# Moving the Toeplitz loads into the last pass, the raw tap loads forward, and the inverse transforms onto one PSUM tile

## The chip, the cores and the metric

One program runs on one core of a Trainium2 chip. The metric is the device time of one execution in microseconds (us). Three runs of the kernel before took 2757.65, 2760.22 and 2761.01 us; the median is 2760.22. A separate execution was recorded by the hardware profiler: it took 2763.0 us, and the span from its first to its last instruction was 2761.2 us.

Engines are named as in the profile: PE is the matrix engine (PEld its weight loads), DVE the vector engine, ACT the scalar engine, POOL the GpSimd engine, SP the engine that only issues DMAs. A row with a q (SPq, ACTq) is the engine's sequencer, which waits and issues.

## The reference, cut to what matters

Four residual layers act on `x` of shape (4, 32, 32, 16): `x = x + conv(_gn(x))` with a group norm `_gn` over 8 groups of 2 channels. The first three layers have the same form:

```
first   = einsum('ijpq,bpqc->bijc', M, inputs)
K       = G as a 3x3 kernel with 16 input and 32*32*16 output channels
shifted = conv3x3(inputs, K).reshape(b, h, w, h, w, f)
diff    = relu(inputs[:, :, :, None, None, :] - shifted)
second  = einsum('ijpq,bpqijc->bijc', Wp, diff)
return first - second
```

So each of the 1024 places (i, j) has nine taps of 16x16 and one 32x32 map of weights. `G` is 9.4 MB and `Wp` 4.2 MB per layer; `Wp` is repeated over 16 channels on its way in. The fourth layer is a convolution with an impulse response:

```
H = rfft2(numerators) / rfft2(denumerator)    # 32 x 32 points here
h = irfft2(H)                                 # the impulse response, 16 x 16 channels
y = irfft2(rfft2(x, 64x64) * (h0 + rfft2(h, 64x64)))[:32, :32]
```

which is a zero-padded linear convolution of the normed input with `h`, plus `h0` at the origin.

## The kernel before, in words

**Conv layers.** The 1024 places of a layer are 128 blocks of 8 places by 16 channels. An iteration is one block for one batch; there are 1536 of them, listed in `order` (L110) in five passes per layer: the first 12 or 16 blocks for batches 0 and 1, the same blocks backwards for batches 2 and 3, the middle blocks for all four batches, then the last 12 or 16 blocks for batches 0 and 1 and, backwards, for 2 and 3. Layer 2 ends with 12 blocks, so its last pass has 24 iterations. An iteration (L740) makes six products that two kinds of pixel share (L704, one iteration ahead), lets ACT copy them beside themselves (L713) and clear the other half of a later tile (L662), adds twelve products of its own (L731), and DVE takes the minimum with zero, multiplies with the block's W and sums, in one instruction (L753). PSUM is four tiles of two banks, used in turn (`pair_psum`, L57). A tile that never served anything else keeps its PE accumulate flags (`full`); one that did has to be written over by two matmuls (L658) before ACT may clear it. The first 24 iterations take another way (`direct`, L671).

**What an iteration needs.** Four blocks make a use (`uses`, `begin`). A use needs an F tile of four taps (L518, three slots f0 to f2), and a taps tile `g` of the others (L574, 1.5 MB, three slots g0 to g2). The latter is made by `other_taps` (L536): SP loads a raw tile (L544; two buffers), POOL subtracts, adds (L510, L549), splits it in a rounded part and the rest (L553, L555; one buffer for the rounded part) and stores both four times over in DRAM (`gd`, L559); `piece_loads` (L568) loads the result into the slot. W tiles are 1 MB for two blocks, in a ring of six (L601 to L629).

**Order of the work.** Every engine runs its instructions in the order in which the program wrote them (`manual_schedule`). The side work is a set of generators. After every iteration `step` (L633) advances each by one `yield`: `todo` has what follows a norm, `tasks` the loads in order of their due times (L586 to L599), which are iteration numbers compared with `now["at"]`. A generator `beside` goes on once a block in a layer's middle pass, and `also` once a block in its last one. SP's DMAs stand in one queue: an issue that waits for a buffer or for another DMA holds up all that is written behind it. The same is true of POOL, which computes as well.

**Layer 3 beside the others.** In the middle pass of layer 0 `impulse_response` (L819) divides the coefficients' transforms and inverts the result in two steps: 64 matmuls into two PSUM tiles (L872) with two ACT copies (L883) and eight stores (L887), then 32 matmuls into two PSUM tiles (L913), two copies (L922), sixteen POOL copies (L928) and a store of `hd`. From `hd` a convolution is a product with Toeplitz tiles k = 0 to 7: one tile is 128 x 4 x 16 x 40 values, 1.31 MB, in which eight groups of 16 partitions hold the same rows shifted; `load_toeplitz` (L942) writes one DMA for each group, odd and even ones on two queues. Tiles 1, 7 and 6 are loaded into a pool of three (`tp`) and tile 0 into one more (`tp2`) in layer 2's middle pass, tile 5 in its last pass, in halves of two W tiles (`late_toeplitz`, L1143). When layer 2 is done, the last norm runs (`norm3`, L1065) and the tail begins (L1158): groups of 16 matmuls (`run`, L1050) over the tiles in the order 1, 0, 7, 6, 5, 4, 3, 2, 0. Tiles 4, 3 and 2 are loaded there, on SP and ACT (L1164 to L1166), each into the `tp` buffer that the matmuls have just left. Beside this, `side` holds the products of pairs of row blocks: ACT copies it out of PSUM (L1169), POOL stores it (L1175) and loads it in another order (L1177, `both`), as it does with the input itself (`xq`, `xd`, `xo`: L1119, L1124, L1159). DVE adds all of it to `xo` (L1181, L1188, L1194), and the two halves of the output are stored (L1200).

Of the kernel before, what the change touches and what calls it, by code (L numbers as in the profile page):

```python
# [7 lines left out]
F32 = mybir.dt.float32  # L8
# [17 lines left out]
GC = 4  # L26
# [11 lines left out]
def conv_stack_kernel(ctx, tc, x, M, W, raw_f, first_g, F, E, h0, coef, cst, dft, idp, idq, out):  # L38
# [497 lines left out]
    def other_taps(q, at):  # L536

        layer, ch = divmod(q, NBLK // GC)
        yield from until(at[0])
        while len(raws) > 1 and stored.get(raws[-2], now["at"]) + 8 > now["at"]:  # L540
            yield
        raws.append(q)
        raw = er.tile([96, 3, 2 * P], F32, tag="raw", name="raw")
        nc.sync.dma_start(out=raw.rearrange("r k n -> r (k n)"), in_=E[layer][ch])  # L544
# [23 lines left out]
    def piece_loads(u, q, slot, free):  # L568

        yield from until(max(free, begin[u] - 12))  # L570
        while q not in stored:
            yield
        gt[q] = t = taps_tile(slot)
        nc.sync.dma_start(  # L574
            out=t.rearrange("p d u s n -> p (d u s n)").bitcast(F32),
            in_=gd[q % len(gd)].rearrange("a k (c d) x -> (a k c) (d x)", d=6),
        )
# [12 lines left out]
    for q in reversed(qs):  # L590
        ready[q] = last = max(min(need[q] - 32, last - 14), 0)
    for q in qs:
        load = max(0, done[-2] + 8, ready[q] - 20)
        at = load, max(ready[q], done[-1] + 1, load + (8 if q else 3))
        done.append(at[1] + 6)
        tasks.append((load, other_taps(q, at)))
    tasks += [(begin[load[0]] - 30, four_taps(n)) for n, load in enumerate(f_plan) if n]
# [10 lines left out]
    def w_free():  # L608
        return any(last is not None and last <= now["at"] for last in ring)
# [209 lines left out]
    def impulse_response():  # L819


        with tc.tile_pool(name="fs", bufs=1) as fs, tc.tile_pool(name="ft", bufs=1) as ft:
            table = fs.tile([P, 2, NF - SOON * P], F32, name="table")
            inv = fs.tile([P, 2, 2, 2 * S], F32, name="inv")
            for h in range(2):
                nc.gpsimd.dma_start(out=table[64 * h : 64 * h + 64], in_=dft)
            nc.gpsimd.dma_start(out=inv, in_=idp)
            H = fs.tile([P, NCH, 2, 2 * P], F32, name="H")
            for ch in range(NCH):
                if ch < SOON:  # L830
                    s = soon[ch]
                else:
                    pab = next_psum()
                    for ri in range(2):
                        coefficient_dft(pab, ab, table[:, :, bass.ts(ch - SOON, P)], ri)
                    s = ft.tile([P, 2, 2, 2 * P], F32, name="s")
# [12 lines left out]
                mul(hr, br, ar)  # L849
                mul(t, bi, ai)  # L850
                nc.gpsimd.tensor_tensor(hr, hr, t, ALU.add)
                mul(hr, hr, d)
                mul(hi, bi, ar)
                mul(t, br, ai)
                nc.gpsimd.tensor_tensor(hi, hi, t, ALU.subtract)
                mul(hi, hi, d)
                yield
                if ch == 0:

                    for ri, one_over in enumerate((d[:2], t[:2])):  # L860
                        nc.vector.reciprocal(one_over, s[:2, 0, ri])
                        mul(H[:2, ch, ri], s[:2, 1, ri], one_over)
                    yield


            pks = [pair_psum() for _ in range(2)]
            for pair in range(2):
                for ri in range(2):
                    for ch in (2 * pair, 2 * pair + 1):
                        for r in range(4):  # L870
                            rows = slice(S * r, S * r + S)
                            nc.tensor.matmul(  # L872
                                pks[r // 2][bass.ts(ch % 2, 64), r % 2, bass.ts(pair, 2 * P)],
                                lhsT=inv[rows, int(ch == 0), ri],
                                rhs=H[rows, ch, ri],
                                start=ri == 0,
                                stop=ri == 1,
                            )

            parts = []  # L880
            for n, pk in enumerate(pks):
                parts.append(H[:, bass.ts(n, 2)].rearrange("p c r n -> p c (r n)"))
                nc.scalar.copy(parts[n], pk)  # L883
            for n, part in enumerate(parts):
                for ch in range(NCH):
                    kx, half = 4 * ch + 2 * n, 64 * (ch % 2)
                    nc.gpsimd.dma_start(  # L887
                        out=td[kx : kx + 2].rearrange("k r p n -> (r p) k n"),
                        in_=part[half : half + 64, :, bass.ts(ch // 2, 2 * P)],
                    )  # L890
                yield


        with tc.tile_pool(name="fs2", bufs=1) as fs:
# [11 lines left out]
                nc.gpsimd.dma_start(out=v[g : g + 32], in_=rows[u])  # L906
            for _ in range(6):
                yield
            pq = [pair_psum() for _ in range(2)]
            quarter = [slice(32 * u, 32 * u + 32) for u in range(4)]  # L910
            for u in range(4):
                for c in range(4):
                    nc.tensor.matmul(  # L913
                        pq[u // 2][quarter[c], u % 2, :],
                        lhsT=inv[quarter[u]],
                        rhs=v[quarter[u], bass.ts(c, 8)].rearrange("g p m -> g (p m)"),
                        start=True,
                        stop=True,
                    )

            for n in range(2):
                nc.scalar.copy(  # L922
                    v[:, bass.ts(n, 16)].rearrange("q (u p) m -> q u (p m)", u=2), pq[n]
                )
            yield
            for u in range(4):
                for c in range(4):
                    nc.gpsimd.tensor_copy(  # L928
                        hs[quarter[u], :, bass.ts(c, 8)],
                        v[quarter[c], bass.ts(u, 8)].rearrange("q p m -> q m p"),  # L930
                    )
                yield
            nc.gpsimd.tensor_tensor(hs[:, :, 0], hs[:, :, 0], h0s, ALU.add)
# [5 lines left out]
                )  # L939
            yield  # L940

    def load_toeplitz(k, *parts, other=nc.gpsimd):  # L942


        n = C * PITCH
        for p in range(8):
            start = 8 + k * TQ * n - p
            for t in parts:
                src = hd[start:]
                size = t.shape[1] * n  # L950
                (nc.sync, other)[p % 2].dma_start(  # L951
                    out=t[p * C : (p + 1) * C].rearrange("i q j r -> i (q j r)"),
                    in_=bass.AP(src.tensor, src.offset, [[HLEN, C], [1, size]]),
                )
# [187 lines left out]

    def late_toeplitz():  # L1143

        half = TQ // 2 * C * PITCH
        parts = []
        for _ in range(2):
            while not w_free():
                yield
            wt = w_tile(len(order)).rearrange("p k m -> p (k m)")  # L1150
            parts.append(wt[:, :half].rearrange("p (q j r) -> p q j r", j=C, r=PITCH))
        ts[held[-1]] = [part[:, q] for part in parts for q in range(TQ // 2)]
        yield from load_toeplitz(held[-1], *parts)

    xs = conv_layer(2, xs, norm3, toeplitz(), late_toeplitz())
    drain()
# [4 lines left out]
    pt = pair_psum()  # L1161
    bank_of.update({1: pt[:, 0], 2: pt[:, 1]})
    for n, slot in enumerate(then):
        if n in (2, 4, 5):  # L1164
            k = {2: 4, 4: 3, 5: last}[n]
            list(load_toeplitz(k, toeplitz_tile(k, late["tp"]), other=nc.scalar))  # L1166
        if n == 3:
            side = junkp.tile([P, 2, S * C], F32, tag="junk", name="side")
            nc.scalar.copy(  # L1169
# [169 lines left out]
```

## Time and profile before

| what | value |
|---|---|
| median of three runs | 2760.22 us |
| profiled execution, and its span | 2763.0 us, 2761.2 us |
| PE, DVE, ACT, POOL busy | 98%, 70%, 64%, 30% of the span |
| one iteration in the steady state, by DVE's starts | 1.69 us |
| Toeplitz tiles 4, 3 and 2 in the tail: first issue, and last landing of each | 2710.09; 2722.94, 2735.60, 2746.08 us |
| DMA, all queues | 652 MB, mean 236 GB/s |

A PE that is 98% busy can still be late: a matmul that runs at half the clock is twice as long, and a tail of 60 us weighs 2% of the whole. So the stages have to be looked at one by one. A row of the timeline gives start, duration, engine, line, operation, tiles as out<-in, and shape; what stands in brackets is the engine's idle time before it and what ended it. A row of the chain of waits gives start, duration and what the end of the program was waiting for just then. Windows give the busy time of each engine in a stretch, the clock that PE was granted (1.00 is all of it), the share of time in which the 16 DMA engines were busy, and the rate.

### The profile page before, as it was taken

Reading aid. Unit: us, or ns where it says so; the run is one execution under the profiler, and the core shown is the slowest. Engines: PE = TensorE matmul, PEld = TensorE weight load, DVE = VectorE, ACT = ScalarE, POOL = GpSimd, SP = SyncE. Lnnn points to the kernel's source line nnn. Section 1 sums busy time; section 2 is a strip of 40 time slices with the busy share of each in tenths; the row PEclk is TensorE's granted clock in tenths of the full one; section 3 lists DMA queues with packets and bytes.
Section 4 is the critical chain, followed back from the end, with each engine's and each line's share of the span. In section 5 each row is a group of like instructions: output and inputs, shape, how many; then the busy total and the mean of one; then the engine's idle time right before and its main releaser. Section 6 shows DMA issues by size and latency. Waiting matters only on the chain.

```text
span 2761.2 us, 81559 instructions
## 1 busy us (share of the span) xinstructions
PE 2708.4 (98%) x34450; PEld 2510.1 (91%) x34450; DVE 1942.4 (70%) x3246; ACT 1775.2 (64%) x3104; POOL 839.2 (30%) x1149
## 2 busy tenths in 40 slices
PE   8899999999999999999999999999999999999997
PEld 5898988999999999999999999999989999999993
DVE  6576766777777777677777777777767777777772
ACT  2566655666666666666666666666666666666660
POOL 5434554322211432332222221333233232322000
PEclk9999999999999999999999999999999999999999
DMA  8887475666675978565666667596856675766515
GB/s 301 290 296 259 174 235 207 255 229 227 236 263 188 325 246 309 197 254 217 227 230 236 246 225 275 189 323 234 326 196 246 221 254 217 268 228 238 233 43 85
DMA packets 134063, 652.14 MB, mean 236 GB/s; under 512 B 18736, under 2 KB 27200, under 8 KB 94528
## 3 DMA queue, kind: packets, MB, share of 16 engines
q1 hardware_dynamic: 84336, 473.63, 46.5%
q0 software_dynamic: 48544, 170.67, 19.2%
q8 instruction: 270, 4.42, 0.7%
q10 hardware_dynamic: 816, 2.62, 0.6%
q14 instruction: 97, 0.79, 0.1%
HBM read 487.24 MB, written 159.61 MB: 234 GB/s over the span
## 4 chain that ended last, share of the span: by engine, by line
PE 85%; DMA 2%; DVE 1%; ACT 0%; issue 0%; ACTq 0%; DVEq 0%; SPq 0%
PE pt L731 65%; PE pt L704 18%; DMA t<-hd 1%; DVE junk L753 1%; PE pt L1056 1%; PE pt L478 1%; DMA w<-in_W_dram 0%; ACT pt L662 0%; DMA g<-gd 0%; PE pt L872 0%; ACT v L922 0%; PE pt L658 0%; ACTq L951 0%; PE pt L913 0%; DVE v L217 0%
## 5 line engine op out<-in xcount | busy, mean ns | idle before, releaser
L753 DVE SCALAR_TENSOR_TENSOR junk<-pt,w 128x1024 f32<-128x1024 f32 x1536 | 1880.3, 1224 | 756.9 <-PE pt L731 715.8
L731 PE MATMUL pt<-f,f 64*128 64x256 f32 x12096 | 1872.6, 376 | 0.0
L731 PE MATMUL pt<-n,g 64*128 64x256 f32 x12096 | 1846.9, 372 | 0.0
L731 PEld LDWEIGHTS pt<-n,g 64*128 64x128 f32 x12096 | 1248.3, 187 | 124.9
L662 ACT COPY pt<-nought_r 128x512 f32<-128x512 f32 x1512 | 889.1, 588 | 552.8 <-DVE junk L753 540.4
L713 ACT COPY pt<-pt 128x512 f32<-128x512 f32 x1512 | 860.5, 569 | 305.1 <-PE pt L704 304.4
L731 PEld LDWEIGHTS pt<-f,f 64*128 64x128 f32 x12096 | 1023.1, 186 | 1.4
L704 PE MATMUL pt<-n,g 64*128 64x256 f32 x9072 | 838.0, 279 | 28.3 <-DMA g<-gd 13.8
L704 PEld LDWEIGHTS pt<-n,g 64*128 64x128 f32 x9072 | 691.0, 186 | 37.9 <-issue 21.0
L510 POOL TENSOR_TENSOR f<-f,cs 128x512 f32<-128x512 f32 x100 | 128.4, 1284 | 1181.1 <-DMA f<-in_F_dram 800.6
L510 POOL TENSOR_TENSOR raw<-raw,cs 96x256 f32<-96x256 f32 x96 | 70.1, 730 | 272.2 <-DMA raw<-in_E_dram 272.0
L549 POOL TENSOR_TENSOR raw<-raw 96x256 f32<-96x256 f32 x192 | 140.1, 730 | 7.8
L753 DVE DVE_READ_ACCUMULATOR junk<-pt,w 128x1 f32 x1536 | 127.5, 83 | 0.0
L555 POOL TENSOR_TENSOR raw<-raw,hi 96x512 fp32r<-96x512 f32 x96 | 122.7, 1278 | 7.1
L559 POOL DMA_DIRECT2D gd<-hi x96 | 66.1, 689 | 0.0
L559 POOL DMA_DIRECT2D gd<-raw x96 | 65.1, 678 | 2.1 <-DMA f<-img 1.6
L553 POOL CAST hi<-raw 96x512 fp32r<-96x512 f32 x96 | 58.3, 607 | 16.8 <-DMA gd<-hi 11.0
L494 POOL DMA_DIRECT2D fd<-ft x48 | 25.1, 530 | 88.5 <-ACT ft L486 82.8
L685 PE MATMUL pt<-first_f,f 64*128 64x512 f32 x192 | 46.8, 601 | 0.0
L1056 PE MATMUL pt<-t,y 128*32 128x512 f32 (+3 forms) x384 | 28.3, 453 | 12.5 <-DMA t<-hd 11.3
L1056 PEld LDWEIGHTS pt<-t,y 128*32 128x32 f32 x384 | 13.5, 113 | 27.3 <-issue 24.4
L394 POOL TENSOR_TENSOR ys<-y 128x64 f32<-128x64 f32 x36 | 9.5, 293 | 87.5 <-DVE y L365 87.5
(140 smaller groups left out, 400.4 us busy)
## 6 DMA issues: line engine op xcount, KB each, us to landing
w<-in_W_dram SPq DMA_DIRECT2D x199, 1024.0 KB, 11.4
g<-gd SPq DMA_DIRECT2D x100, 1536.0 KB, 10.1
gd<-hi POOLq DMA_DIRECT2D x96, 768.0 KB, 6.9
gd<-raw POOLq DMA_DIRECT2D x96, 768.0 KB, 8.9
f<-in_F_dram SPq DMA_DIRECT2D x100, 512.0 KB, 4.0
raw<-in_E_dram SPq DMA_DIRECT2D x96, 288.0 KB, 13.0
mt<-in_M_dram SPq DMA_DIRECT2D x12, 512.0 KB, 14.7
w<-in_M_dram SPq DMA_DIRECT2D x12, 512.0 KB, 15.3
```

The lines of the kernel that those rows point to most:

```text
L510: engine.tensor_tensor(v, v, m.unsqueeze(1).to_broadcast([v.shape[0], v.shape[1], C]), ALU.subtract)
L549: nc.gpsimd.tensor_tensor(raw[:, 0], raw[:, 0], raw[:, k], ALU.add)
L553: nc.gpsimd.tensor_copy(hi, both)
L555: nc.gpsimd.tensor_tensor(lo, both, hi.bitcast(F32), ALU.subtract)
L559: nc.gpsimd.dma_start(out=gd[q % len(gd)][:, k].rearrange("a c n -> c a n"), in_=whole.unsqueeze(1).to_broadcast([96, 4, 4 * P]),)
L662: nc.scalar.copy(here, nought.unsqueeze(2).to_broadcast(list(here.shape)))
L685: nc.tensor.matmul(pt[:, half, px], lhsT=taps_of(u, blk, half, (0, 2)) if k == 2 else f[rows, k, at], rhs=rhs, start=k == 0, stop=k == 2,)
L704: nc.tensor.matmul(of_half(pt, half, 0), lhsT=taps_of(u, blk, half, (dy, dy), 0), rhs=ni[rows, dy : dy + 4, 2], start=False, stop=dy == 2, ...
L713: nc.scalar.copy(v[:, :, 1], v[:, :, 0])
L731: nc.tensor.matmul(of_half(pt, half, k), lhsT=w, rhs=rhs, start=False, stop=k == 1 and j == 2, skip_group_check=True,)
L753: nc.vector.scalar_tensor_tensor(junk, pt.rearrange("p h m -> p (h m)"), 0.0, wts[w_at[i]][:, blk % 2, :], ALU.min, ALU.mult, accum_out=ac ...
L1056: nc.tensor.matmul(rows.rearrange("n (j r) -> n j r", j=C)[:, :, 8 * cc :], lhsT=y(cc).rearrange("p q b -> p (q b)"), rhs=ts[k][q][:, :, : ...
```

## The change: what it does

1. The Toeplitz tiles 4, 3 and 2 are no longer loaded in the tail. `late_toeplitz` loads four tiles in the last pass: 5 and 3 in halves of W tiles, 4 and 2 in taps slots, the first two once the first of the pass's three uses is over, the other two once the second is. They go out on SP and POOL, none on ACT.
2. `other_taps` may load a raw tile 5 steps, not 8, after the store of the one before the last, and the due times are worked out with 5 and 6 for 8. `piece_loads` holds a taps load back until 5 steps after its store was written, or 3 before its use. So both kinds of load change places with others in SP's queue.
3. Both inverse transforms work through one PSUM tile at a time: the tile that is next in turn (`next_psum`), half of the matmuls, the copy, two `yield`s, then the other half. The first half of each goes to an SBUF tile of its own (`part`, `inverse`), since the source is still needed.

```
 other_taps:
-        while len(raws) > 1 and stored.get(raws[-2], now["at"]) + 8 > now["at"]:
+        while len(raws) > 1 and stored.get(raws[-2], now["at"]) + 5 > now["at"]:
 piece_loads:
-        while q not in stored:
+        while q not in stored or now["at"] < min(stored[q] + 5, begin[u] - 3):
             yield
 due times:
-        load = max(0, done[-2] + 8, ready[q] - 20)
-        at = load, max(ready[q], done[-1] + 1, load + (8 if q else 3))
+        load = max(0, done[-2] + 5, ready[q] - 20)
+        at = load, max(ready[q], done[-1] + 1, load + (6 if q else 3))
 impulse_response, first inverse:
-            pks = [pair_psum() for _ in range(2)]
...
+            parts = [ft.tile([P, 2, 2 * 2 * P], F32, tag="s", name="part")]
+            parts.append(H[:, 2:].rearrange("p c r n -> p c (r n)"))
             for n, part in enumerate(parts):
+                pk = next_psum()
+                for pair in range(2):
+                    for ri in range(2):
+                        for ch in (2 * pair, 2 * pair + 1):
+                            for r in range(2 * n, 2 * n + 2):
...
+                nc.scalar.copy(part, pk)
+                for _ in range(2):
+                    yield
 second inverse:
-            pq = [pair_psum() for _ in range(2)]
...
+            both = [fs.tile([P, 2, 8, 64], F32, name="inverse"), v[:, 16:].rearrange("q (u p) m -> q u p m", u=2)]
+            for n, to in enumerate(both):
+                pq = next_psum()
...
+                nc.scalar.copy(to.rearrange("q u p m -> q u (p m)"), pq)
+                for _ in range(2):
+                    yield
 late_toeplitz:
+        def in_w(k):
+            half = TQ // 2 * C * PITCH
+            parts = []
+            for _ in range(2):
+                wt = w_tile(len(order)).rearrange("p k m -> p (k m)")
+                parts.append(wt[:, :half].rearrange("p (q j r) -> p q j r", j=C, r=PITCH))
+            ts[k] = [part[:, q] for part in parts for q in range(TQ // 2)]
+            return parts
+
+        def in_taps(k, use):
+            slot = {q: slot for _, q, slot, _ in g_plan}[uses[use][0]]
+            t = gn.tile([P, 3 * GC * 2 * P], F32, tag=f"g{slot}", name="t")
+            t = t[:, : TQ * C * PITCH].rearrange("p (q j r) -> p q j r", j=C, r=PITCH)
+            ts[k] = [t[:, q] for q in range(TQ)]
+            return [t]
+
+        for use, *ks in ((-3, *after[2:4]), (-2, after[4], last)):
+            yield from until(begin[len(uses) + use + 1])
+            for k, parts in zip(ks, (in_w(ks[0]), in_taps(ks[1], use))):
+                yield
+                list(load_toeplitz(k, *parts))
 tail:
-        if n in (2, 4, 5):
-            k = {2: 4, 4: 3, 5: last}[n]
-            list(load_toeplitz(k, toeplitz_tile(k, late["tp"]), other=nc.scalar))
```

More of the change, by code (lines that the diff above doesn't have):

```diff
@@ L835, in impulse_response @@
                         coefficient_dft(pab, ab, table[:, :, bass.ts(ch - SOON, P)], ri)
-                    s = ft.tile([P, 2, 2, 2 * P], F32, name="s")
+                    s = ft.tile([P, 2, 2, 2 * P], F32, tag="s", name="s")
                     with_ones(s, pab, ones[:, ch])
@@ L863, in impulse_response @@
                     yield
-            pks = [pair_psum() for _ in range(2)]
[L867 to L883, printed above, removed]
-            for n, part in enumerate(parts):
+            parts = [ft.tile([P, 2, 2 * 2 * P], F32, tag="s", name="part")]
+            parts.append(H[:, 2:].rearrange("p c r n -> p c (r n)"))
+            for n, part in enumerate(parts):
+                pk = next_psum()
[3 more added lines that the diff above has]
+                            for r in range(2 * n, 2 * n + 2):
+                                rows = slice(S * r, S * r + S)
+                                nc.tensor.matmul(
+                                    pk[bass.ts(ch % 2, 64), r % 2, bass.ts(pair, 2 * P)],
+                                    lhsT=inv[rows, int(ch == 0), ri],
+                                    rhs=H[rows, ch, ri],
+                                    start=ri == 0,
+                                    stop=ri == 1,
+                                )
+                nc.scalar.copy(part, pk)
+                for _ in range(2):
+                    yield
                 for ch in range(NCH):
@@ L908, in impulse_response @@
                 yield
-            pq = [pair_psum() for _ in range(2)]
             quarter = [slice(32 * u, 32 * u + 32) for u in range(4)]
[L911 to L925, printed above, removed]
+            both = [fs.tile([P, 2, 8, 64], F32, name="inverse"), v[:, 16:].rearrange("q (u p) m -> q u p m", u=2)]
+            for n, to in enumerate(both):
+                pq = next_psum()
+                for u in range(2):
+                    for c in range(4):
+                        nc.tensor.matmul(
+                            pq[quarter[c], u],
+                            lhsT=inv[quarter[2 * n + u]],
+                            rhs=v[quarter[2 * n + u], bass.ts(c, 8)].rearrange("g p m -> g (p m)"),
+                            start=True,
+                            stop=True,
+                        )
+                nc.scalar.copy(to.rearrange("q u p m -> q u (p m)"), pq)
+                for _ in range(2):
+                    yield
             for u in range(4):
@@ L929, in impulse_response @@
                         hs[quarter[u], :, bass.ts(c, 8)],
-                        v[quarter[c], bass.ts(u, 8)].rearrange("q p m -> q m p"),
+                        both[u // 2][quarter[c], u % 2].rearrange("q p m -> q m p"),
                     )
@@ L940, in impulse_response, with load_toeplitz @@
             yield
-    def load_toeplitz(k, *parts, other=nc.gpsimd):
+    def load_toeplitz(k, *parts):
         n = C * PITCH
@@ L950, in load_toeplitz @@
                 size = t.shape[1] * n
-                (nc.sync, other)[p % 2].dma_start(
+                (nc.sync, nc.gpsimd)[p % 2].dma_start(
                     out=t[p * C : (p + 1) * C].rearrange("i q j r -> i (q j r)"),
@@ L1143, in late_toeplitz @@
     def late_toeplitz():
[L1145 to L1148, printed above, removed]
+        def in_w(k):
[15 more added lines that the diff above has]
+            for k, parts in zip(ks, (in_w(ks[0]), in_taps(ks[1], use))):
                 yield
[L1150 to L1153, printed above, removed]
+                list(load_toeplitz(k, *parts))
     xs = conv_layer(2, xs, norm3, toeplitz(), late_toeplitz())
```

## The prediction

> **What bounds the kernel now.** The page first: busy times, and the chain that ended last by engine.
>
> ```profile
> PE 2708.4 (98%) x34450; PEld 2510.1 (91%) x34450; DVE 1942.4 (70%) x3246; ACT 1775.2 (64%) x3104; POOL 839.2 (30%) x1149
> ...
> PE 85%; DMA 2%; DVE 1%; ACT 0%; issue 0%; ACTq 0%; DVEq 0%; SPq 0%
> ```
>
> PE sets the pace, 1.69 us an iteration. No part of the change touches that pace, so only places where PE falls short of it can give or cost anything. DVE has one long instruction for each iteration, so its starts show these places: the intervals above 1.69 add up to 88 us over the three layers. Three of the places, and the tail, are where the change works. The chain over the tail:
>
> ```profile
> 2711.45 11.49 DMA t<-hd
> 2722.94 0.02 issue
> 2722.96 12.64 DMA t<-hd
> 2735.60 0.02 issue
> 2735.62 10.46 DMA t<-hd
> ```
>
> For 35 us the end hangs on the loads of tiles 4, 3 and 2, not on PE. The timeline of the same stretch tells what PE loses by it (a first wait of 1.05 us, at 2722, stands above these rows):
>
> ```profile
> 2735.84 8.33 PE L1056 MATMUL pt<-t,y 128*32 128x512 f32 x96 [8.15 <-DMA t<-hd]
> ...
> 2745.82 1.42 DVE L1181 TENSOR_TENSOR xo<-xo,both 128x512 f32<-128x512 f32 x2 [39.23 <-DMA both<-sd]
> ...
> 2746.32 10.97 PE L1056 MATMUL pt<-t,y 128*32 128x512 f32 x160 [2.15 <-DMA t<-hd]
> ```
>
> DVE's L1181 also waits until 2745.82, for `both`, whose loads and stores lie between those of `t`. Next, timelines of the first inverse transform and of the one wait for taps (DVE's intervals there are 4.4 to 5.6 us, and 16.6):
>
> ```profile
> 363.50 0.98 PE L704 MATMUL pt<-n,g 64*128 64x256 f32 x6 [2.01 <-ACT pt L662]
> ...
> 369.04 0.62 PE L704 MATMUL pt<-n,g 64*128 64x256 f32 x6 [2.00 <-ACT pt L662]
> ```
>
> ```profile
> 116.92 1.21 PE L704 MATMUL pt<-n,g 64*128 64x256 f32 x6 [12.82 <-DMA g<-gd]
> ```
>
> Two of four PSUM tiles away leave PE, ACT and DVE to wait for each other in turn. The taps come late because SP's queue was held up; its own timeline:
>
> ```profile
> 63.46 18.50 SPq L574 DMA_DIRECT2D g<-gd  x2
> 82.06 0.37 SPq L544 DMA_DIRECT2D raw<-in_E_dram  x1
> ...
> 109.82 0.34 SPq L574 DMA_DIRECT2D g<-gd  x1
> ```
>
> The raw load at 82.06 stood behind a taps load that waited until 81.62 for its stores to land. From it follow POOL's work at 91.59, the stores at 100.33, landed at 109.75, and the taps load at 109.82, landed at 116.67.
>
> **Part 1, the tail.** Removed: 24 issues (12 SP, 12 ACT) behind the last iteration. Added in the last pass: 32 more DMAs, 16 on SP and 16 on POOL. Price of a POOL issue: tile 5's from 2673.60 to 2677.18 take 0.48 to 0.51 us each while DVE runs; SP's are 0.3 to 0.4. Nothing that PE needs is behind them on either queue: POOL's next is `xd`, SP's the output. Waits added: W tiles of the first two uses (DVE through at 2673.3 and 2686.9) and their taps slots. Tile 5 took from 2673.3 to 2682.6; the others took 10.5 to 12.9 us. In line that gives tile 4 at 2694, 3 at 2705, 2 at 2717. PE wants them at 2722, 2726 and 2733, so their loads are covered, with 16 us to spare for the last. PE then goes from 2713.31 without a break: three stretches of 64 at 4.33 (from the start of one at 2713.31 to that of the next at 2717.64), 96 at 6.50 by the same rate, and 10.97: 2743.8, against 2757.3. That is 13.5 us: 11.35 of idle (1.05, 8.15, 2.15), 1.8 of half clock, rest rounding. The 1.13 for the copy of `side` stays.
>
> What is late next is `both`. Its chain on POOL is now behind tile 2: `xd` at worst 2717, stores 3 us and landing 2.4, `xo`, four issues of `sd` (2.14) and, without the loads of `t` beside, landings of 3 to 4 us each: `both` by 2730 to 2735. L1181 and the five of L1188 (1.42 and 3.5) have to be done by 2744: 4 to 9 us of slack. Bounds: 13.5 if it holds; if `both` landed at 2745.8 as before, L1181, L1188 and L1194 would end at 2751.5: 6 us. I take 13.5, since 3.9 MB leave that stretch.
>
> **Part 3, the inverse transforms.** Before, DVE's starts go from 356.35 to 374.86 in four intervals, 11.75 us over four paces, and from 422.17 to 439.82: 10.89. Together 22.6. Now there are four blocks with one PSUM tile each. The nearest row is the forward transform of coefficients, which already works in that way (L833): 333.24 to 337.64, 2.7 us lost:
>
> ```profile
> 337.64 1.23 DVE L753 SCALAR_TENSOR_TENSOR junk<-pt,w 128x1024 f32<-128x1024 f32 x1 [3.17 <-PE pt L731]
> ```
>
> It has 8 matmul rows and 1.4 us of ACT; the new blocks have 1.3 us (half of 2.6) or 1.1 us of PE, and one copy of 1.0. So 2.9 each, 11.6 in all, a gain of 11.0. Bounds: 1.5 each (PE and the writing-over alone) gives 16.6, 5.4 each (half of an old pair) gives 1. The later store of `hd` costs nothing: its first reader is two layers away.
>
> **Part 2, the early order.** In the built programs few instructions of SP change places after iteration 110, and the taps loads none after 193; so this part acts in the first 200 us. There the raw load of 60.75 moves up behind the taps load of 47.10, the one of 82.06 to about 62.5, ahead of the second taps load, and the images for batches 2 and 3 go ahead of the first taps load. Step by step, with the durations of the rows: stores of the raw at 47.5 issued at 62 to 63.4 (before 72.2), landed at 71; raw of 62.5 landed at 70; POOL's seven image issues and four steps (3.7, 4.4) and the second seven; its stores issued at 82 to 83 (before 101), landed at 92; taps load to 99. PE, without its 12.8 and with the 4.7 lost at 59.0 to 67.0 (images of batch 3 landing at 64.86), would want them at 99.2. All of it is worth 19.5: DVE's 47th iteration came at 120.78, and would come at 101.2.
>
> But the DMA engines then have to move as much in less time. In two windows (stretch, busy time of PE, PEld, DVE, ACT, POOL, then PE's clock, the DMA share, GB/s) they had idle time to give:
>
> ```profile
> 70.00:80.00 10.00, 10.00 (x135) 10.00 (x133) 7.31 (x12) 7.24 (x13) 6.48 (x11) 1.00 0.79 232
> 80.00:90.00 10.00, 10.00 (x135) 10.00 (x133) 7.40 (x14) 6.95 (x12) 3.69 (x7) 1.00 0.80 233
> ```
>
> From 63.5 to 116.7 they were busy for 46 us of 53 by these and the neighbouring windows (shares 0.98, 0.89, 0.84, 0.90). Some 6 of these served loads and stores that are now behind (an F, a raw, part of a W and of the next stores), so 40 remain: taps at 103, 3.8 late, a gain of 15.7. Then I take off 2 for W and taps loads that meet the raw work pulled forward until 200 us, where the share was 0.9. So 13.5; bounds 4 (the DMA engines save only their 7 idle us, and 3 come back later) and 19.5.
>
> A rule beside it: the Trainium skill's "DMA: Bandwidth & Descriptors" (Specifications) puts the limit from HBM at about 358 GB/s for a core. By that rate the 16 MB of 60 to 120 us would need 45 us, not 60, and this part would give 15. The trace does not agree with it as a limit: 130 to 140 us moved 407 GB/s. Another row speaks against reckoning by rates at all: 2720 to 2730 had a share of 1.04 at 184 GB/s.
>
> A rule against part 1: "SBUF — State Buffer" (its box on the DVE blocking DMAs of the GpSimd queue) says that POOL cannot write descriptors while DVE holds their shared port in a fast mode. Tile 5's eight POOL issues of 0.5 us under DVE's L753 show no such block; with an L753 of 1.22 us ahead of each of 24 issues they would take 41 us, to 2715, which hardly changes the sum.
>
> **Sum.** 13.5 + 11.0 + 13.5 = 38 us. The profiled execution took 2763.0 (span 2761.2, 1.8 around it), so it would take 2725. The median is 2.8 below that execution: 2722.
>
> **Rivals.** (a) The early gain gets lost in DMA time: with 4 for part 2, 28.5 us gained, 2732. For it: shares of 0.8 to 1.0 there. Against: over 20% idle in 70 to 90, and the chain of single waits. (b) The tail's last loads and `both` collide, part 1 gives 6: 2730. (c) Part 1 does not do what it says: loads held until the last iteration, since a W tile's or slot's last reader is later than I read it. Gain 0 there: 2735. Against: tile 5 lands at 2682 already. (d) Slower: the raw work pulled forward puts each use's taps or W behind gd's stores, and PE waits at each of the ten uses from iteration 48 to 192, with half the clock after each. At 4 us and 1.7 (the one after 116.92 cost that) each, 57 lost against 38 won: 2779. It decides from 3.8 us a use. Against: a use lasts 27 us and moves 5.8 MB, 215 GB/s, less than the 299 and 306 of 160 to 200.
>
> **Chances.** Forecast 0.50, (a) 0.28, (b) 0.07, (c) 0.06, (d) 0.07, nothing 0.02. The likeliest is 2722. The range takes in part 3 from 5 to 13, (a) to (c), and 46 us gained at best: 2714 to 2745. Measurement can tell 0.2%, 5.5 us: faster 0.91, same 0.02, slower 0.07.
>
> **What will show it.** Right: no `t<-hd` in the chain of the tail, and PE's L1056 without a break from the copy of `side`; four DVE intervals of about 4.6 us, in place of eight, at L875 and L915; the wait of L704 for `g<-gd` under 5 us at iteration 47. Wrong: L1181 as the last wait of the tail; new waits of L704 or L753 for `g` or `w` between 100 and 350 us; an idle PE in the last pass.

## The result: 20 us faster, and the profile after

The changed kernel took 2739.6 us (median of four runs, 2736.8 to 2740.7) against 2759.7 for the kernel before (median of four, 2757.7 to 2761.0): a ratio of 0.9927, with a 95% interval of 0.9914 to 0.9941, so 20 us faster (16 to 24). Forecast were 2722 us and 38 us of gain; the range, 2714 to 2745, holds the time. The profiled execution took 2736.8 us, with a span of 2734.9. Against the profiled execution before, 2763.0, that is 26 us, and these 26 can be told apart by place:

| place | forecast | from trace to trace |
|---|---|---|
| tail, from the last L753 to the end: 62.6 us before, 49.0 after | 13.5 | 13.6 |
| the two inverse transforms: time lost by DVE's intervals over 1.69 us, 22.6 before, 11.2 after | 11.0 | 11.4 |
| first 48 iterations | 13.5 | 2.4 |
| a stop in the last pass, at iteration 1532 | 0 | -1.0 |

The page after, busy times of PE to POOL and the chain that ended last by engine:

```profile
PE 2703.1 (99%) x34450; PEld 2507.4 (92%) x34450; DVE 1941.5 (71%) x3246; ACT 1775.3 (65%) x3104; POOL 846.9 (31%) x1165
...
PE 86%; DVE 1%; ACT 0%; DMA 0%; issue 0%; DVEq 0%; ACTq 0%
```

The 2% that DMA had in the chain are gone. The chain of waits over the tail shows why; a row is start, duration, and what the end waited for:

```profile
2699.55 1.02 ACT side L1177
2700.57 0.04 issue
2700.61 30.40 PE pt L1055 x448
2731.01 0.02 issue
2731.03 0.42 DVE xo L1202
```

From the copy of `side` on PE goes through its 448 matmuls without a break. DVE's timeline of the same stretch, then that of the first inverse transform in the kernel before and of both transforms in the changed one (the number ahead of an arrow in brackets is the idle time before the row):

```profile
2709.67 1.42 DVE L1189 TENSOR_TENSOR xo<-xo,both 128x512 f32<-128x512 f32 x2 [15.78 <-DMA both<-sd]
...
2731.03 0.75 DVE L1202 TENSOR_TENSOR xo<-xo,pt 128x256 f32<-128x256 f32 x2 [2.23 <-PE pt L1055]
```

```profile
361.59 1.23 DVE L753 SCALAR_TENSOR_TENSOR junk<-pt,w 128x1024 f32<-128x1024 f32 x1 [4.01 <-PE pt L731]
...
367.13 1.22 DVE L753 SCALAR_TENSOR_TENSOR junk<-pt,w 128x1024 f32<-128x1024 f32 x1 [4.31 <-PE pt L731]
...
371.96 1.23 DVE L753 SCALAR_TENSOR_TENSOR junk<-pt,w 128x1024 f32<-128x1024 f32 x1 [3.60 <-PE pt L731]
...
374.86 1.23 DVE L753 SCALAR_TENSOR_TENSOR junk<-pt,w 128x1024 f32<-128x1024 f32 x1 [1.67 <-PE pt L731]
```

```profile
358.99 1.23 DVE L753 SCALAR_TENSOR_TENSOR junk<-pt,w 128x1024 f32<-128x1024 f32 x1 [3.77 <-PE pt L731]
...
382.48 1.22 DVE L753 SCALAR_TENSOR_TENSOR junk<-pt,w 128x1024 f32<-128x1024 f32 x1 [3.67 <-PE pt L731]
...
445.65 1.22 DVE L753 SCALAR_TENSOR_TENSOR junk<-pt,w 128x1024 f32<-128x1024 f32 x1 [2.79 <-PE pt L731]
...
461.50 1.22 DVE L753 SCALAR_TENSOR_TENSOR junk<-pt,w 128x1024 f32<-128x1024 f32 x1 [2.79 <-PE pt L731]
```

`both` has landed 21 us before PE's last matmul ends. Four DVE intervals (5.00, 4.90, 4.02 and 4.02 us, an idle of 0.46 in each being the usual one) have taken the place of eight, of 2.8 to 5.6 us. The place that disappoints is the wait for taps at iteration 46, counted from 0. PE's timeline, then SP's queue and POOL's:

```profile
114.73 1.21 PE L704 MATMUL pt<-n,g 64*128 64x256 f32 x6 [7.86 <-DMA f<-in_F_dram]
```

```profile
82.27 0.33 SPq L544 DMA_DIRECT2D raw<-in_E_dram  x1
...
102.60 0.34 SPq L574 DMA_DIRECT2D g<-gd  x1
103.04 1.99 SPq L518 DMA_DIRECT2D f<-in_F_dram  x1
105.54 1.37 SPq L544 DMA_DIRECT2D raw<-in_E_dram  x1
```

```profile
69.75 0.71 POOL L510 TENSOR_TENSOR raw<-raw,cs 96x256 f32<-96x256 f32 x1 [0.62 <-DMA raw<-in_E_dram]
76.42 0.54 POOL L444 DMA_DIRECT2D f<-img  x1 [5.96 <-DMA img<-ye]
...
80.18 1.55 POOL L549 TENSOR_TENSOR raw<-raw 96x256 f32<-96x256 f32 x2
...
89.49 0.70 POOL L559 DMA_DIRECT2D gd<-hi  x1
91.54 0.68 POOL L559 DMA_DIRECT2D gd<-raw  x1 [1.35 <-DMA f<-img]
...
101.52 0.68 POOL L559 DMA_DIRECT2D gd<-hi  x1
102.18 0.68 POOL L559 DMA_DIRECT2D gd<-raw  x1
```

The name in PE's bracket is the wait that came last by the records; the taps landed at 114.38, 0.35 us before PE went on. The fourth raw tile landed at 69.67, as forecast (70). But POOL, after its first step on it, writes the loads of the images next, and these wait 5.96 us for the images' own stores. The tile's stores go out at 89.5 and 91.5 and land at 98.4 and 102.4. The taps load behind them takes 11.8 us, beside an F, a raw and a W load and the stores of the fifth tile, issued at 101.5 and 102.2.

### The profile page after: what moved, and what is told of

The parts are those of the page before. It is cut to its first block, busy times and chain, and to the rows that moved or that the text cites. A ratio compares the mean times of both kernels' runs of the same rounds, so it can differ in the third digit from the quotient of the medians.

```text
span 2734.9 us, 81577 instructions
## 1 busy us (share of the span) xinstructions
PE 2703.1 (99%) x34450; PEld 2507.4 (92%) x34450; DVE 1941.5 (71%) x3246; ACT 1775.3 (65%) x3104; POOL 846.9 (31%) x1165
## 4 chain that ended last, share of the span: by engine, by line
PE 86%; DVE 1%; ACT 0%; DMA 0%; issue 0%; DVEq 0%; ACTq 0%
PE pt L731 66%; PE pt L704 18%; PE pt L1055 2%; PE pt L478 1%; DVE junk L753 0%; DMA g<-gd 0%; ACT pt L662 0%; PE pt L875 0%; PE pt L658 0%; PE pt L915 0%; ACT part L882 0%; ACT H L882 0%; ACT side L1177 0%; ACT v L922 0%; ACT inverse L922 0%
## 5 line engine op out<-in xcount | busy, mean ns | idle before, releaser
L753 DVE SCALAR_TENSOR_TENSOR junk<-pt,w 128x1024 f32<-128x1024 f32 x1536 | 1879.7, 1224 | 744.7 <-PE pt L731 707.7
L753 DVE DVE_READ_ACCUMULATOR junk<-pt,w 128x1 f32 x1536 | 126.7, 82 | 0.0
L555 POOL TENSOR_TENSOR raw<-raw,hi 96x512 fp32r<-96x512 f32 x96 | 122.7, 1279 | 7.1
L685 PEld LDWEIGHTS pt<-first_f,f 64*128 64x128 f32 x192 | 18.3, 186 | 18.0 <-issue 10.9
L444 POOL DMA_DIRECT2D n<-img x48 | 25.0, 525 | 15.1 <-DMA gd<-hi 6.2
```

The lines of the kernel that those rows point to most:

```text
L685: nc.tensor.matmul(pt[:, half, px], lhsT=taps_of(u, blk, half, (0, 2)) if k == 2 else f[rows, k, at], rhs=rhs, start=k == 0, stop=k == 2,)
L753: nc.vector.scalar_tensor_tensor(junk, pt.rearrange("p h m -> p (h m)"), 0.0, wts[w_at[i]][:, blk % 2, :], ALU.min, ALU.mult, accum_out=ac ...
```

## Experiments

Two theories stood for the early part. Order: POOL's and SP's queues hold the taps up, and another order brings the rest of the 13.5 us. DMA: the engines that move the data are full from 60 to 115 us, so what comes earlier only makes something else late. First the three parts one by one.

**Part 1 alone**: item 1 of the change, put into the kernel before; an excerpt.

```
+        for use, *ks in ((-3, *after[2:4]), (-2, after[4], last)):
...
-        if n in (2, 4, 5):
-            k = {2: 4, 4: 3, 5: last}[n]
-            list(load_toeplitz(k, toeplitz_tile(k, late["tp"]), other=nc.scalar))
```

> The kernel before with part 1 alone: tiles 4, 3 and 2 loaded in the last pass. Theory A (the three parts add up, and each is worth what the trace of the changed kernel shows at its place): 13.6 us of the tail less the 1.0 us that PE stands at 2681, so 12.6 us faster than before, about 2747; no load of t in the chain of the tail, and the stop of about 1 us in the last pass is there too. Rival B (the stop at 2681 has nothing to do with these loads but comes from another part): no such stop, 13.6 us faster. Rival C (the tail gains only since the other parts let the last pass start from other buffers): under 10 us.

Measured: 2746.8 us against 2762.5, ratio 0.9942 (0.9928 to 0.9956), 12 to 20 us faster. From the last L753 to the end it took 49.0 us, 13.6 less than before. Chain of waits:

```profile
2708.57 30.40 PE pt L1056 x448
2738.97 0.02 issue
2738.99 0.42 DVE xo L1203
```

The same 30.40 us: the tail's gain belongs to part 1 alone, and rival C falls. The stop of 1 us in the last pass is not there, so these loads do not bring it by themselves.

**Part 3 alone**: item 3 of the change, put into the kernel before; an excerpt.

```
-            pks = [pair_psum() for _ in range(2)]
...
+                pk = next_psum()
```

> The kernel before with part 3 alone: one PSUM tile at a time in both inverse transforms. Theory A: four DVE intervals of 4.0 to 5.0 us in place of eight of 4.4 to 5.6, 22.6 us lost becomes 11.2, so 11.4 us faster, about 2748. Rival C (a part of what is won there is lost again further on, at a load that then comes late): the four intervals as said, but under 8 us in the time and a new wait between 450 and 700 us.

Measured: 2751.3 us against 2762.5, ratio 0.9960 (0.9945 to 0.9976), 7 to 15 us faster. The intervals are 4.99, 4.90, 4.02 and 4.02 us, 11.2 lost: theory A. Over the next layers this profile loses some of its lead at layers' ends (more below), but at no load moved by part 3.

**Part 2 alone**: item 2 of the change; it is four lines, of which the first two are:

```
-        while len(raws) > 1 and stored.get(raws[-2], now["at"]) + 8 > now["at"]:
+        while len(raws) > 1 and stored.get(raws[-2], now["at"]) + 5 > now["at"]:
...
-        while q not in stored:
+        while q not in stored or now["at"] < min(stored[q] + 5, begin[u] - 3):
```

> The kernel before with part 2 alone: other due times of raw, taps and images. Theory A (the gain is lost in the stretch of 60 to 115 us itself): 2.4 us faster as in the trace of the changed kernel, about 2757; taps for iteration 47 land at about 114 us, not at 99 to 103. Rival B (the forecast's: the part gives 13.5 us, and only the other parts take it away): about 2746, taps landed by 103.

Measured: 2757.6 us against 2762.5, ratio 0.9979 (0.9968 to 0.9991), 2.5 to 9 us faster. In its trace PE still waits 8.73 us for taps at iteration 46:

```profile
116.13 1.22 PE L704 MATMUL pt<-n,g 64*128 64x256 f32 x6 [8.73 <-DMA g<-gd]
```

They landed at 115.8, 17 us later than the 99 that the forecast's chain gave: what is missing was lost in part 2 itself, without the others. (The trace is that of the slowest of the twelve executions, 2768.8 us, but in the changed kernel, whose trace is of the fastest, they landed at 114.4.)

**The changed kernel without part 2** puts the same question from the other side; its edit is the reverse of the last one.

> The changed kernel without part 2 (the early order as before; parts 1 and 3 stay). Part 2 gained 5.7 us alone (interval 2.5 to 8.8 by the ratio) and 2.4 us in the trace of the changed kernel. Theory A (the parts are independent): 2 to 6 us slower than the changed kernel, about 2741. Rival (part 2 is worth nothing beside the others): the same time as the changed kernel.

Measured: 2740.9 us against 2760.4, ratio 0.9923 (0.9910 to 0.9937). Its iteration 48 begins at 122.7 us, as before (122.8); in two traces of the changed kernel at 120.4 and 121.0. In time the two can't be told apart from call to call, since the changed kernel's ratios are 0.9927 and 0.9909, so the times decide for neither of the two theories. So part 2 is worth about 2 us by the traces, and 2.5 to 9 by the run alone.

**POOL's steps in one go**, first test of the order. Only the `yield`s between the steps on the fourth tile go, so that all four and the stores stand ahead of the images' loads:

```
 other_taps, after each of the four steps:
-        yield
+        if q != 3:
+            yield
```

> The changed kernel, in which POOL's four steps for the fourth raw tile are written in one go, ahead of the seven images' loads that wait for the images' own stores. In the trace of the changed kernel POOL stands 5.96 us between its first and second step, and its stores go out at 89.5 and 91.5. Theory O (order: what is late is POOL, held up by the images' issues): stores go out at about 80, taps land before 105, the wait of 7.9 us at iteration 47 goes to 0 to 2, with the half clock after it: 8 to 10 us faster than the changed kernel, about 2730. Theory D (DMA: the engines are busy at 0.9 to 1.07 of 60 to 110 us, so what comes earlier is served later): stores go out at about 80 as well, but taps or the images for batches 2 and 3 land late, and the time stays within 3 us of the changed kernel, or gets longer by a longer stop at iterations 22 to 24.

Measured: 2736.3 us, ratio to the kernel before 0.9897 (0.9878 to 0.9916). That is 3 to 8 us better than the two ratios of the changed kernel, with intervals that overlap. The stores went out at 75.4 and 76.1 and had landed by 89.3, which is earlier than even the forecast had them. Yet the DVE interval at iteration 46 fell to 7.4 us only (11.6 before this edit). SP's queue:

```profile
94.87 0.90 SPq L444 DMA_DIRECT2D n<-img  x2
98.37 0.35 SPq L624 DMA_DIRECT2D w<-in_W_dram  x1
99.42 0.34 SPq L578 DMA_DIRECT2D g<-gd  x1
100.14 0.33 SPq L518 DMA_DIRECT2D f<-in_F_dram  x1
```

The taps load now stands 10 us behind images and a W load whose places in the queue have to come free, and lands at 109.5. Windows of that stretch (columns as before: PE, PEld, DVE, ACT, POOL, PE's clock, DMA share, GB/s):

```profile
80.00:90.00 10.00, 10.00 (x135) 10.00 (x133) 7.26 (x13) 6.81 (x13) 2.13 (x5) 1.00 1.04 326
90.00:100.00 10.00, 10.00 (x135) 10.00 (x132) 7.40 (x14) 6.81 (x13) 7.56 (x13) 1.00 1.00 185
100.00:110.00 10.00, 6.21 (x81) 6.04 (x77) 5.64 (x10) 4.46 (x8) 2.27 (x3) 1.00 0.97 366
```

Both theories got half: the order was worth 5 us in the trace (iteration 48 begins at 115.5, not 120.4), and behind it stand full DMA engines.

**The fifth tile's stores held**, alone and with POOL's steps in one go, and the changed kernel again beside them:

```
+        if q == 4:
+            yield from until(48)
         for k, t in enumerate((hi, lo)):
```

> The changed kernel once more, beside the next three, for its time on the same chip and a second trace. Its ratio to the kernel before was 0.9927, so about 2740. Theory A: what differs between two traces lies where PE waits for DMAs (iterations 22 to 24, 46, and at layer ends), and the inverse transforms and the tail repeat to 0.1 us.

> The changed kernel, in which the stores of the fifth raw tile (issued at 101.5 and 102.2 in its trace, right beside the taps load of 102.6 that PE waits for) are held until iteration 48. Theory K (the taps load took 11.8 us since it ran against those stores): it lands 4 to 5 us earlier, at about 109, and the kernel is 4 to 5 us faster than the changed one. Rival L (it ran against the F, raw and W loads issued in the same 5 us, and the stores count for little): it lands at 112 to 114, less than 2 us.

> POOL's four steps in one go as before in this series, and the fifth tile's stores held until iteration 48. In the trace with POOL's steps in one go the taps load was issued at 99.4, held by SP's queue, and landed at 109.5 with the stores issued at 100.9 and 101.6. Theory K: it lands at about 105, the DVE interval of 7.4 us at iteration 46 becomes about 3, 4 us faster than with POOL's steps alone (about 2732). Rival L: within 2 us of that.

Measured, on one chip: the changed kernel 2736.8 us, ratio 0.9909 (0.9890 to 0.9927); stores held 2735.8, 0.9908 (0.9892 to 0.9925); both 2731.9, 0.9893 (0.9878 to 0.9908). In the trace with the stores held the taps took 6.5 us, from 103.4 to 109.9, not 11.8, as theory K has it for the landing. PE's waits in the two:

```profile
110.24 1.21 PE L706 MATMUL pt<-n,g 64*128 64x256 f32 x6 [4.29 <-DMA g<-gd]
```

```profile
106.70 0.82 PE L710 MATMUL pt<-n,g 64*128 64x256 f32 x6 [1.14 <-DMA f<-in_F_dram]
```

Yet the time with the stores held alone is within 1 us of the changed kernel's: what its trace won (5 us at iteration 48) does not show in the median of its five runs, which reach from 2732 to 2742, so K's 4 to 5 us in time stay unconfirmed. The two edits together do show, with 4.9 us in the medians.

**The images first.** PE also stands for the images at iterations 22 to 24: DVE's intervals there were 2.3, 7.8 and 3.0 us. POOL's last image load waits for the stores ahead of it, so these were to be held:

```
+        if q == 1:
+            yield from until(17)      # in the second run: until(19)
         for k, t in enumerate((hi, lo)):
```

> The same, and the second raw tile's stores (POOL, 47.3 and 48.0) held until iteration 17, behind the last loads of the images for batches 2 and 3. In the traces POOL's last image load stood 5.9 to 6.7 us, until the first of those stores had landed, eight DMAs of POOL being on their way, and PE stood for n<-img at iterations 22 to 24 (7.5 us). Theory Q (the queue's eight places and the stores ahead set the images' landing): the last image is issued by 54 and lands at about 60, the interval at iteration 23 falls from 7.5 to 3, 4 us faster. Rival F (the DMA engines are full, share 1.00 from 50 to 60, so the images land at 64 in any case, and the stores come late behind them): within 2 us, or slower by a later stop at iterations 32 to 47.

> The run before it of this name held nothing: the stores were written at iteration 17 already, so it was the same kernel in effect as the one with POOL's steps in one go and the fifth tile's stores held. Now the second raw tile's stores are held until iteration 19, and POOL's seven loads of the images for batch 3 stand ahead of them. Theory Q (POOL's eight places and the stores ahead set the images' landing): the last image is issued by 52 and lands at about 60, the DVE interval of 7.8 us at iteration 23 falls to 3 or 4, some 4 us faster, about 2728. Rival F (the DMA engines are full there, or the stores only come late behind the images): the images land at 63 or later, or the 4 us come back as a longer stop at iterations 24 to 47; within 2 us of the kernel without the hold.

> POOL's steps in one go and the fifth tile's stores held, once more, as the one to compare the held images with on the same chip: 2732, as it was twice (2731.9 and 2732.1).

With 17 the edit moved nothing, since the stores were written at iteration 17 in any case: 2732.1 us, ratio 0.9894 (0.9878 to 0.9911), is a second measurement of the kernel without it. With 19 the loads did change places: 2734.3 us, 0.9908 (0.9893 to 0.9924), beside 2733.2, 0.9901 (0.9888 to 0.9915), without. POOL's queue without and with:

```profile
46.73 0.70 POOL L565 DMA_DIRECT2D gd<-hi  x1 [0.38 <-DMA gd<-raw]
47.50 0.68 POOL L565 DMA_DIRECT2D gd<-raw  x1
48.17 0.52 POOL L444 DMA_DIRECT2D f<-img  x1
48.68 1.04 POOL L444 DMA_DIRECT2D n<-img  x2
49.71 1.11 POOL L444 DMA_DIRECT2D f<-img  x2
50.81 0.53 POOL L444 DMA_DIRECT2D n<-img  x1
56.53 0.53 POOL L444 DMA_DIRECT2D n<-img  x1 [5.19 <-DMA gd<-hi]
```

```profile
49.58 1.04 POOL L444 DMA_DIRECT2D n<-img  x2
50.61 0.70 POOL L567 DMA_DIRECT2D gd<-hi  x1
51.30 0.68 POOL L567 DMA_DIRECT2D gd<-raw  x1
```

POOL's last image is issued 6 us earlier, and the interval at iteration 23 goes from 7.1 to 5.0 us, since SP's last image still lands at 63.1 (64.4 without the edit). The 2 us come back at iteration 46, where the interval goes from 5.5 to 7.3. Iteration 48 begins at 113.8 us with and at 113.6 without: rival F, to 0.2 us.

**The taps load ahead of the images**, the last test of the order:

```
-        yield from until(max(free, begin[u] - 12))
+        yield from until(max(free, begin[u] - (16 if q == 3 else 12)))
-        while q not in stored or now["at"] < min(stored[q] + 5, begin[u] - 3):
+        while q not in stored or now["at"] < min(stored[q] + (1 if q == 3 else 5), begin[u] - 3):
```

> POOL's steps in one go and the fifth tile's stores held, as before, and SP issues the taps load ahead of the last seven images' loads and a W load. In the kernel without that, its stores landed at 87.7, SP issued it at 96.4 to 98.1 and it landed at 106.4 to 107.7, the DMA engines being busy for 43 to 44 us of the 43 to 44 us from 63.5 on. Theory F (what the DMA engines have to move up to iteration 48 takes its 43 us in any order, and images and W are needed there too): taps land by 99, but PE then waits for n<-img, f<-img or w at iterations 46 to 48 until 104 or later; the lead over the kernel before at iteration 48 stays between 8 and 12 us, the time within 2 us of 2732. Rival O (only the order is wrong, and PE needs nothing but the taps): the wait at 46 is gone (interval 1.69), lead 13 us or more at iteration 48, about 2729.

Measured: 2734.2 us, ratio 0.9896 (0.9880 to 0.9913). The median is 2.2 us above 2732, just over what theory F allowed, and 5 above rival O's 2729; the ratio is among those of the kernel without the edit (0.9893, 0.9894, 0.9901). So nothing was gained that shows, but the trace can't carry the verdict. That execution (2743.5, the longest of its four) had DVE intervals of 11.1, 5.0 and 2.3 us at iterations 22 to 24, with a DMA share of only 0.43 from 60 to 70 us, and everything after that is shifted; its taps landed at 112.7, not 99. That the order could still win the last microsecond or two is left open.

The windows from 63.5 us to the landing of the taps for iteration 48 put the early runs in one view: the kernel before, the changed one, the stores held, both edits.

```profile
63.50:116.70 53.20, 39.45 (x506) 38.91 (x506) 28.49 (x47) 27.67 (x49) 27.41 (x40) 0.91 0.84 256
```

```profile
63.50:114.40 50.90, 42.41 (x506) 42.07 (x506) 28.48 (x47) 28.72 (x51) 24.95 (x41) 0.91 0.96 286
```

```profile
63.50:109.90 46.40, 41.09 (x506) 40.52 (x506) 28.50 (x47) 29.72 (x55) 24.97 (x41) 0.96 0.95 276
```

```profile
63.50:106.40 42.90, 40.99 (x506) 40.79 (x506) 28.12 (x46) 29.55 (x53) 24.65 (x40) 0.96 1.00 302
```

Length by share gives the DMA engines' work: 44.7 us before, 48.9 in the changed kernel, 44.1 with the stores held, 42.9 with both. (In the second trace of the changed kernel the work was 49.7.) With both edits the share of that stretch is 1.00: no idle time is left to win.

## Why the prediction was right, and where 11 us went

**Right: direction, bound and two of three terms.** PE's pace did not move; PE 99% says it too. The tail gave 13.6 where 13.5 were forecast, and the stretch from the copy of `side` to PE's last matmul 30.40 us where the forecast's end, 2743.8 against 2713.31, made it 30.5. The inverse transforms lost 11.2 us where 11.6 were forecast: 3.3, 3.2, 2.3 and 2.3, against 2.9 each. (The intervals before are called 4.4 to 5.6 us in the prediction; two of the eight were 2.9 and 2.8. Its sum of 22.6 has them right.) Rivals (b) and (c) fell with the tail's chain; (d) fell too, since every DVE interval over 2.2 us between iterations 48 and 192 stands in the kernel before as well, apart from the two of the inverse transform.

**Sized wrong, without harm: the tiles "in line".** Tiles 4, 3 and 2 were to land at 2694, 2705 and 2717. They landed at 2680, 2689 and 2697, beside each other. `both` followed at 2709.65, not at 2730 to 2735.

**Wrong: the early term.** It was to give 13.5 and gave 2.4 and 1.8 in the two traces of the changed kernel. Two steps failed. "Its stores issued at 82 to 83 (before 101), landed at 92": they were issued at 89.5 and 91.5 and landed by 102.4. The step counted POOL's image issues by their own duration. It left out that these wait for the images' stores, which land at 76.3 (5.96 us), and for a free place among POOL's DMAs (four waits from 86 to 92 us, 3.4 us together); with POOL's steps in one go the same stores had landed by 89.3. And "some 6 of these served loads and stores that are now behind (an F, a raw, part of a W and of the next stores), so 40 remain": the DMA engines were busy for 48.9 us, not 40. The next stores, those of the fifth tile, were not behind the taps load but ahead of it, issued 1.1 and 0.4 us before; holding them took 4.8 us of that work out, and the load from 11.8 to 6.5 us. What was argued as a gain of order ended as rival (a) has it, in DMA time, though by another price: 2.4, not 4.

The two edits together, which mend both steps, start iteration 48 earlier than the kernel before by 12.1, 9.1 and 9.1 us in their three traces. That is what the early term could have given; 13.5 was still too much, since 42.9 to 44.5 us of DMA work, not 40, lie ahead of the taps.

**The range held, but not for the reasons that it was given.** 2739.6 is 17.6 us above the likeliest time and slower than rivals (a), (b) and (c) each had it alone (2732, 2730, 2735). Of the gain that is missing, 11 us are the early term and 1 us is the stop in the last pass. The other 6 lie between what the two traces differ by (26) and what the medians do (20): the profile of the kernel before, 2763.0, lies above its four timed executions, and that of the changed kernel is the fastest of its four. The range was wide for part 3 and for the rivals; that it also covered this is luck. Of the signs named beforehand, the four intervals and the tail without loads of `t` came. The wait for taps under 5 us did not (7.86), and one sign of being wrong did: PE stood in the last pass, for the 1 us at iteration 1532.

**The rule weighed beside it.** The Trainium skill's "DMA: Bandwidth & Descriptors" (Specifications) has about 358 GB/s from HBM for a core. In the stretch with a share of 1.00 (both edits), 42.9 us moved 302 GB/s, 13.0 MB. By that rate they would take 36 us, and the trace does not agree in either direction: the stretch is slower, and the window of 100 to 110 us above, with 366 GB/s, is faster. The share of busy time was what ran out, not the rate. The block that the Trainium skill's "SBUF — State Buffer" describes (its box on the GpSimd queue) did not show either: POOL's issues in the last pass took 0.48 to 0.51 us each. Whether DVE's L753 runs in the fast mode that the box speaks of, no run here shows.

**What does not add up to the microsecond.** Traces give 26 us, medians 20 and, in the second measurement, 25. Besides the early waits it is the stops after iterations 510 and 1022, at the layers' ends, that differ between executions: their DVE intervals run from below 2.4 to 5.4 and from 2.4 to 6.1 us over the fourteen traces, whatever the kernel.

**The better version.** POOL's steps in one go and the fifth tile's stores held took 2731.9, 2732.1 and 2733.2 us, ratios 0.9893, 0.9894 and 0.9901 to the kernel before. On the chip where the changed kernel took 2736.8 it was 4.9 us faster by the medians, with executions of 2729.8 to 2733.3 against 2733.1 to 2738.2.

## What to carry to other kernels

A transfer that is moved earlier brings its followers with it: list what is issued within the microseconds before it and beside it, on every queue, and hold back what nobody needs yet. Before forecasting a gain from another order of loads, multiply the stretch by its DMA share; most of that work stays (41 to 50 us in the traces here, in whatever order), and only the idle rest (here 8.5 us of 53) and what can be put behind the waited-for load is there to win. A chain of issues on POOL is as slow as the slowest thing it waits for, so its steps are costed by the landings ahead of them, not by their durations.

## What the runs showed that was not expected

- **Eight DMAs on their way.** POOL's ninth DMA stands until the first of the eight ahead of it has landed (the 5.19 us above, after `gd<-hi`), and SP's likewise: in the changed kernel an image load at 55.56 followed the landing of a taps load at 55.54. In the tail of the kernel before, where SP and ACT take turns, the eight are counted over both: in the prediction's chain ACT's load of 2722.96 waits for the landing of that of 2711.45, eight loads back, four on each queue. By the traces' records each such issue waits for the semaphore (a counter that instructions raise and wait for) that its own landing will raise, one of eight for POOL and one of eight for SP and ACT together. So the eight is a matter of the program as built; whether the queues have a limit of their own is not shown. Either way an order of issues is also an order of landings, eight apart.
- **A full share says little of the rate.** Shares of 1.00 and 0.97 went with 185 and 366 GB/s in neighbouring windows of one kernel.
- **The old form of the inverse transforms varied from trace to trace**: it lost 22.6 us in the kernel before, 16.5 with part 1 alone and 23.4 with part 2 alone. The one with one PSUM tile at a time lost 11.2 in ten traces of eleven, and 12.7 in the one without part 2. The tail does the same: 62.6, 63.0 and 64.4 us in the three traces with the old loads, 49.0 in each of the eleven with the new ones.
- **A stop of 1.0 us at iteration 1532** stands in two of eleven traces with the loads in the last pass (the changed kernel's first and the one without part 2). Its cause was not found.
